# Local attention with score tiles of two PSUM banks, and one POOL add for the rotation

## The chip, the cores and the metric

The kernel runs on one core of a Trainium2 chip. The time of a run is the device time of that core in microseconds (us), and kernels are compared by the median of several runs. The profile is one more execution of the same program, recorded by the hardware profiler. Its engines are PE (matrix products, with PEld for the weight loads beside it), DVE (vector engine), ACT (scalar engine, functions such as Exp and Ln) and POOL (the second vector engine). Each engine works through its own list of instructions in the order in which they were written, and semaphores make one engine wait for another. PSUM, where PE writes, has eight banks of 512 float32 numbers in each of 128 partitions. SBUF holds everything else.

## The reference

The reference is a network of many different blocks on an input of 16 sequences of 256 tokens with 128 channels, 4096 tokens in all. One block, local attention followed by a gated feed-forward net, occurs twice with the same weights, and each occurrence has two layers (`DEPTH`). So local attention is computed four times. Cut to what matters here:

```python
HEADS, DIM_HEAD, WINDOW, QK_SCALE = 8, 64, 64, 8.0

def _layer(x, wqkv, qs, ksc, wo, ...):
    h = shift_token(x)                 # half of the channels come from the token before
    q, k, v = split(h @ wqkv)          # 8 heads of 64 each
    q = l2norm(q) * qs                 # q / clip(norm(q), 1e-12)
    k = l2norm(k) * ksc
    q, k = rotary_xpos(q, k)           # q*cos*scale + rotate_half(q)*sin*scale, k with 1/scale
    o = local_attention(q, k, v)
    x = x + o @ wo
    ...                                # shift, layer norm, feed-forward

def rotate_half(x):
    x1, x2 = jnp.split(x, 2, axis=-1)
    return jnp.concatenate([-x2, x1], axis=-1)

def local_attention(q, k, v):          # windows of 64 tokens, each sees itself and the one before
    ...
    sim = jnp.einsum('bhwid,bhwjd->bhwij', bq * QK_SCALE, bk)
    sim = jnp.where((i < j) | (i > j + WINDOW) | (j == -1), -max, sim)
    return jnp.einsum('bhwij,bhwjd->bhwid', softmax(sim), bv)
```

## The kernel before

The program runs its blocks one after the other. A local layer is `local_attend` (line 3358) followed by `local_ffn`. I number the four calls of `local_attend` layers 1 to 4 in order of time.

**Tiles and slots.** The 4096 tokens are cut into 32 *tiles* of 128 tokens (`NTILE`), so two tiles make one sequence. The work on a tile makes q, k and v ready. The attention itself goes by *slots*, also 32: slot m is sequence m // 2 with four of the eight heads. Eight chunks of 512 tokens (`NCH`) carry the residual, the norm and the output.

**What is done for a tile n.**
- `project`: PE multiplies the tile with the q and the k weights into two `w` banks of PSUM. ACT squares both banks into `sq` (`sq<-ps`). DVE multiplies each bank with the cosine and the sine table (`t<-ps,tab`, four instructions), into `t1` and `t2`. The tables already hold the signs and the scales.
- `rotate`: DVE sums the squares over each head into `ss`, 16 numbers a token (`ss<-sq`), and raises them to at least 1e-24, which is a maximum with a constant tile `least` (`ss<-ss,least`, called the *floor* below). POOL adds `t2` to `t1` with the halves of each head exchanged, in two instructions, one for each half (`t<-t,t`, lines 3408 and 3409).
- `unit`: ACT takes Ln and then Exp of `ss` in place (`ss<-ss`), which gives one over the norm. POOL multiplies `t1` with it (`t<-t,ss`).
- `turn`: PE transposes `t1` into `w` banks (line 508), ACT copies them into `qkt`, and PE makes v in another `w` bank, which ACT copies to SBUF (`v<-ps`).

**What is done for a slot m.**
- `score`: four banks from the group `s`. PE puts the mask into the last two by a product with the identity (line 504), and eight products (line 3447) fill all four. The first two banks hold the scores against the first key tile, 384 numbers each, the other two those against the second, 256 each. DVE takes the minimum of the first two with the mask `see` into `pt` (line 531, two instructions, 384 wide), and ACT takes the exponentials of the other two into `pu` (`pu<-ps`, two instructions, 256 wide).
- `first_weights`: ACT takes the exponential of `pt` in place.
- `weigh`: PE multiplies the weights with v into an `o` bank and sums them by a product with ones (line 3485). The sums go to `pd`, the unused half of the last score bank of the slot that comes next (`spare[3]`); the last slot takes banks for itself.
- `inverse` and `divide`: ACT takes Ln and Exp of `pd`, which gives one over the sum (`rd`), and DVE multiplies the `o` bank with it into `ot`.

`out` multiplies `ot` with the output weights and adds it to the residual, once in four slots. `chunk_steps` has the layer norm of the next part and the token shift of chunks not yet needed (`shift`, three POOL instructions).

**The order.** It is written out by hand. One loop runs m from -9 to 37, and each turn of it calls, where the index is in range: `score(m)`, `weigh(m-1)`, `out`, `turn(m+2)`, `first_weights(m)`, `rotate(m+4)`, `inverse(m-1)` and `divide(m-1)`, `unit(m+4)`, `chunk_steps(m)`, `project(m+5)`. So in one turn a tile is projected five turns before, rotated four turns before and turned two turns before the slot of the same number. The turns with m below 0 have no score yet: I call them the *lead-in* of a layer. In it only tiles are prepared. From slot 0 on each turn has a whole slot as well.

**The banks.** `self.share(w=3, s=4, o=1)` divides the eight banks: three for projections, transposes, v and outputs, four for scores, one for the weighted sum. A tile's next use waits for the instructions that read or wrote it last. `t1` has three buffers, `t2` and `sq` one, `ss` three, `pt`, `pu` and `rd` two.

The helper names in the profile: `tt` is line 531 (DVE), `gt` line 534 (POOL), `act` line 528, `mm` line 504, `tr` line 508. A line there says how an engine was called, not who called it; so the groups are told apart by their tiles.

Of the kernel before, what the change touches and what calls it, by code (L numbers as in the profile page):

```python
# [11 lines left out]
F32, BF16, I32 = mybir.dt.float32, mybir.dt.bfloat16, mybir.dt.int32  # L12
SP = mybir.EngineType.SP
AF = mybir.ActivationFunctionType
ALU = mybir.AluOpType
AX = mybir.AxisListType

P = 128
B, T, C = 16, 256, 128
# [3 lines left out]
NTILE = NT // P  # L23
# [468 lines left out]
class Net:  # L492
# [16 lines left out]

    def bank(self, tag="ps"):  # L510
        return self.psum.tile([P, 512], F32, tag=tag, name="ps", bufs=self.banks[tag])

    @contextmanager
    def share(self, **banks):
# [1135 lines left out]
class Fast(Net):  # L1650
# [1707 lines left out]
    def local_attend(self, w, z, hs, last):  # L3358
# [6 lines left out]
        with ExitStack() as st:  # L3365
            p = self.stage(st, "l1", 1)
# [15 lines left out]
            made, rot, qkt, val, weights, sums, outs, steps, spare = {}, {}, {}, {}, {}, {}, {}, {}, []  # L3382
# [19 lines left out]
            def rotate(n):  # L3402
                sq, t1, t2 = made.pop(n)
                ss = p.tile([P, 16], F32, tag="ss", name="ss", bufs=3)
                nc.vector.tensor_reduce(ss, sq.rearrange("p i (h d) -> p (i h) d", h=8), AX.X, ALU.add)
                self.tt(ss, ss, least, ALU.max)
                a, b = (t.rearrange("p i h a d -> p (i h) a d") for t in (t1, t2))
                for k in range(2):
                    self.gt(a[:, :, k], a[:, :, k], b[:, :, 1 - k], ALU.add)
                rot[n] = t1, ss  # L3410

            def unit(n):
                t1, ss = rot[n]

                self.act(ss, ss, AF.Ln, scale=2.0**20)
                self.act(ss, ss, AF.Exp, scale=-0.5)
                t3 = t1.rearrange("p i h a d -> p (i h) (a d)")
                self.gt(t3, t3, ss[:, :, None].broadcast_to([P, 16, 64]), ALU.mult)

            def turn(n):  # L3420
                b, t = divmod(n, 2)
                if t == 0:
                    qkt[b] = p.tile([P, 2, 4, T], F32, tag="qkt", name="qkt", bufs=2)
                t1, _ = rot.pop(n)
                for i in range(2):
                    pt = self.bank("w")
                    for g in range(4):
                        self.tr(pt[:, g * P : g * P + P], t1[:, i, 2 * g : 2 * g + 2])
                    self.act(qkt[b][:, i, :, t * P : t * P + P], pt.rearrange("p (g t) -> p g t", g=4), AF.Copy)
                pv = self.bank("w")  # L3430
                self.mm(pv, hs[:, n * P : n * P + P], w["qkv"][:, 1024:])
                val[n] = p.tile([P, 512], F32, tag="v", name="v", bufs=6)
                self.act(val[n], pv, AF.Copy)

            def score(m):


                b, hg = divmod(m, 2)
                qt, kt = qkt[b][:, 0], qkt[b][:, 1]
                ps = [self.bank("s") for _ in range(4)]  # L3440
                for bank in ps[2:]:
                    self.mm(self.bt(bank[:, :T]), identb, self.twice(masked), stop=False)

                def product(a, i, t, out):
                    rows, g = slice(64 * a, 64 * a + 64), 2 * hg + i
                    wide = 192 - 64 * t
                    nc.tensor.matmul(
                        out, kt[rows, g, t * P : t * P + P], qt[rows, g, t * P : t * P + wide],
                        start=(i, t) == (0, 0), stop=i == 1, skip_group_check=t == 0,
                    )  # L3450

                for i, t, bank, at in ((0, 0, 0, 0), (1, 0, 0, 192), (0, 1, 2, 0), (1, 1, 2, P)):
                    for a in range(2):
                        product(a, i, t, ps[bank + a][:, at : at + 192 - 64 * t])
                pt = p.tile([P, 2, 384], F32, tag="pt", name="pt", bufs=2)
                pu = p.tile([P, 4, P], F32, tag="pu", name="pu", bufs=2)
                for a in range(2):
                    self.tt(
                        pt[:, a].rearrange("p (i t) -> p i t", i=2), ps[a][:, :384].rearrange("p (i t) -> p i t", i=2),
                        self.twice(w["see"]), ALU.min,  # L3460
                    )
                for a in range(2):
                    self.act(pu[:, a::2], self.bt(ps[2 + a][:, :T]), AF.Exp)
                weights[m] = pt, pu
                spare[:] = ps

            def first_weights(m):
                pt = weights[m][0]
                flat = pt.rearrange("p a t -> p (a t)")
                self.act(flat, flat, AF.Exp)  # L3470

            def weigh(m):


                b, hg = divmod(m, 2)
                pd, po = spare[3][:, T:] if m < NTILE - 1 else self.bank("s")[:, T:], self.bank("o")
                pt, pu = weights.pop(m)
                for half in (0, 1, -1):
                    for t in range(2):
                        wide = 192 - 64 * t  # L3480
                        for r in range(4):
                            i, a = divmod(r, 2)
                            d = (4 * hg + r) * 64 + 32 * half
                            at = max(half, 0) * T + t * P
                            nc.tensor.matmul(
                                (pd if half < 0 else po)[32 * r : 32 * r + 32, at : at + wide],
                                self.ones64[:, :32] if half < 0 else val[2 * b + t][:, d : d + 32],
                                pu[:, r] if t else pt[:, a, i * wide : i * wide + wide],
                                start=t == 0 and half < 1, stop=t == 1 and half != 0, skip_group_check=True,
                            )  # L3490
                sums[m] = pd, po

            def inverse(m):
                pd, po = sums[m]
                rd = p.tile([P, T], F32, tag="rd", name="rd", bufs=2)
                self.act(rd, pd, AF.Ln)
                self.act(rd, rd, AF.Exp, scale=-1.0)
                sums[m] = po, rd

            def divide(m):  # L3500
                b, hg = divmod(m, 2)
                if m % 4 == 0:
                    outs[b // 2] = p.tile([P, 4, CH], F32, tag="ot", name="ot", bufs=1)
                po, rd = sums.pop(m)
                at = b % 2 * T
                self.tt(
                    outs[b // 2][:, 2 * hg : 2 * hg + 2, at : at + T], po.rearrange("p (g t) -> p g t", g=2),
                    self.twice(rd), ALU.mult,
                )

            def out(c):
                pz = self.bank("w")
                ot = outs.pop(c)
                for g in range(4):
                    self.mm(pz, w["wo"][:, g * C : g * C + C], ot[:, g], start=g == 0, stop=g == 3)
                zs = z[:, self.chunk(c)]
                self.tt(zs, zs, pz, ALU.add)

            def within(n, many):
                return 0 <= n < many  # L3520
# [18 lines left out]
                            steps[1] = self.norm_of_half(p, "w", w, hs[:, self.chunk(c)])  # L3539
                        steps[1][i]()  # L3540

            with self.share(w=3, s=4, o=1), self.tc.manual_schedule():
                self.logs()
                for m in range(-9, NTILE + 6):
                    if within(m, NTILE):
                        score(m)
                    if within(m - 1, NTILE):
                        weigh(m - 1)
                    c, rest = divmod(m - 5, 4)
                    if rest == 0 and 0 <= c < NCH:  # L3550
                        out(c)
                    if within(m + 2, NTILE):
                        turn(m + 2)
                    if within(m, NTILE):
                        first_weights(m)
                    if within(m + 4, NTILE):
                        rotate(m + 4)
                    if within(m - 1, NTILE):
                        inverse(m - 1)
                        divide(m - 1)  # L3560
                    if within(m + 4, NTILE):
                        unit(m + 4)
                    chunk_steps(m)
                    if within(m + 5, NTILE):
                        project(m + 5)
# [278 lines left out]
```

## Time and profile before

| | |
|---|---|
| median of 4 runs | 4235.99 us (4234.45 to 4236.53) |
| profiled execution | 4233.97 us, span 4232.2 us from its first to its last instruction |
| mean granted clock of PE over the span | 0.951 |
| busy over the whole span | PE 91%, PEld 52%, DVE 60%, ACT 55%, POOL 44% |

The four layers of local attention lie at these places. A window of slots runs from the score of slot 2 to the end of the last score, slot 31; a lead-in window from DVE's first products of the layer to the score of slot 1.

| layer | lead-in, us | PE busy there | POOL busy there | slots 2 to 31, us | PE busy there |
|---|---|---|---|---|---|
| 1 | 116.50 to 142.25 | 17.88 of 25.75 | 22.51 | 149.13 to 394.70 | 238.91 of 245.57 |
| 2 | 470.50 to 496.30 | 18.55 of 25.80 | 21.27 | 503.15 to 737.50 | 231.49 of 234.35 |
| 3 | 1108.80 to 1134.50 | 18.55 of 25.70 | 21.43 | 1141.30 to 1386.90 | 238.94 of 245.60 |
| 4 | 1462.70 to 1488.30 | 19.28 of 25.60 | 21.20 | 1495.20 to 1729.50 | 231.44 of 234.30 |

Layers 1 and 3 take 11 us longer for their slots than 2 and 4, because their `chunk_steps` carry the first norm of the next layer too.

How the profile is read: a group of instructions is one line, engine and operation, written `out<-in` by the program's tile names, with partitions x elements. In a timeline each row has the start in us, the length, the engine and line, the operation; "x2" is a run of two equal instructions whose lengths are given together, and a bracket at the end is the idle time ahead of it and what ended it. In a list of waits a row gives the idle time, the number of waits and the longest, after the instruction that waited and the one that released it. Windows give the busy time of each engine in a stretch, the number of instructions in brackets, the granted clock (1.00 is full speed) and the share of time in which DMA engines worked.

### The profile page before, as it was taken

How to read it: one execution, taken by the hardware profiler on the slowest of the kernel's cores; microseconds unless marked ns; L12 is line 12 of the kernel's file. 1: busy time of each engine (PE TensorE's matmuls, PEld its weight loads, DVE VectorE, ACT ScalarE, POOL GpSimd, SP SyncE). 2: the span in 40 equal slices, each digit the busy share in tenths (PEclk: the TensorE clock that was granted, in tenths of full speed). 3: DMA queues.
4: the chain of work that ended last, by engine and by line, in shares of the span. 5: the costliest groups of instructions: out<-in, count | busy, mean ns of one | idle time of the engine just before them, and what ended most of it. 6: DMA issues, size and time to landing. Idle time of an engine off the chain costs nothing. (4 is left out here: it accounts for less than half of the span.)

```text
span 4232.2 us, 73089 instructions
## 1 busy us (share of the span) xinstructions
PE 3861.2 (91%) x28742; PEld 2203.3 (52%) x28742; DVE 2557.2 (60%) x4503; ACT 2315.7 (55%) x4485; POOL 1855.0 (44%) x1632
## 2 busy tenths in 40 slices
PE   7999999998899999985989879888999999899978
PEld 3555466464465466454965459543444344455333
DVE  4775676464577477473346633555777677486374
ACT  6666466555766466652456634344555454774532
POOL 4763465232565266225433434454555455321251
PEclk9999999988999999996999979999999999999979
DMA  1800000000000000004920049100000000000000
GB/s 61 344 2 1 11 1 2 20 1 1 20 1 1 3 1 2 1 11 143 318 70 12 16 161 313 42 19 16 1 1 1 3 1 6 10 2 19 6 0 21
DMA packets 78400, 176.38 MB, mean 42 GB/s; under 512 B 12606, under 2 KB 39108, under 8 KB 77920
## 3 DMA queue, kind: packets, MB, share of 16 engines
q1 hardware_dynamic: 65568, 148.40, 10.2%
q0 software_dynamic: 9120, 18.51, 1.2%
q8 instruction: 229, 3.75, 0.4%
q10 hardware_dynamic: 3360, 4.72, 0.3%
q14 instruction: 123, 1.01, 0.1%
HBM read 118.28 MB, written 54.20 MB: 41 GB/s over the span
## 5 line engine op out<-in xcount | busy, mean ns | idle before, releaser
L528 ACT ACTIVATE pt<-ps 128x512 f32<-128x512 f32 x640 | 339.9, 600 | 326.1 <-PE ps L504 324.6
L504 PE MATMUL ps<-hb,w 128*128 128x512 f32 (+1 forms) x960 | 461.3, 614 | 4.0 <-issue 3.3
L504 PE MATMUL ps<-w,hb 128*128 128x512 f32 (+2 forms) x896 | 399.8, 567 | 25.5 <-DVE t L531 19.4
L534 POOL TENSOR_TENSOR t<-t,t 128x512 f32<-128x512 f32 x256 | 319.7, 1270 | 160.2 <-DVE t L531 139.6
L531 DVE TENSOR_TENSOR t<-ps,tab 128x512 f32<-128x512 f32 x512 | 317.6, 681 | 82.5 <-ACT sq L528 79.0
L534 POOL TENSOR_TENSOR t<-t,ss 128x1024 f32<-128x1024 f32 x128 | 243.6, 1903 | 192.4 <-ACT ss L528 191.2
L504 PEld LDWEIGHTS ps<-hb,w 128*128 128x128 f32 (+1 forms) x960 | 179.2, 191 | 260.8 <-issue 223.6
L528 ACT ACTIVATE qkt<-ps 128x512 f32<-128x512 f32 x256 | 140.5, 595 | 290.8 <-PE ps L508 290.8
L531 DVE TENSOR_TENSOR u<-u,ps 128x384 f32<-128x384 f32 (+1 forms) x206 | 121.8, 595 | 277.0 <-PE ps L504 117.4
L531 DVE TENSOR_TENSOR ot<-ps,rd 128x512 f32<-128x512 f32 (+2 forms) x224 | 143.2, 639 | 202.7 <-ACT rd L528 202.7
L534 POOL TENSOR_TENSOR nsq<-ha 128x512 f32<-128x512 f32 x112 | 123.5, 1103 | 317.7 <-ACT ha L528 302.0
L504 PEld LDWEIGHTS ps<-w,hb 128*128 128x128 f32 x896 | 155.3, 192 | 178.4 <-issue 121.6
L534 POOL TENSOR_TENSOR both<-pt 128x1024 f32<-128x1024 f32 x64 | 151.3, 2364 | 199.6 <-DVE pt L531 163.9
L504 PE MATMUL ps<-nsq,ct 128*128 128x512 f32 x368 | 203.0, 634 | 30.2 <-POOL nsq L534 25.7
L504 PE MATMUL ps<-ot,w 128*128 128x512 f32 x448 | 213.6, 611 | 16.8 <-DVE ot L531 9.0
L504 PE MATMUL ps<-xt,w 128*128 128x128 f32 x1704 | 221.1, 280 | 1.6 <-ACT xt L528 1.5
L2199 POOL DMA_INDIRECT back<-y,x x142 | 139.1, 980 | 184.3 <-ACT y L528 61.0
L504 PE MATMUL ps<-u,w 128*128 128x512 f32 (+1 forms) x448 | 215.4, 605 | 3.4 <-POOL u L534 3.4
L504 PEld LDWEIGHTS ps<-xt,w 128*128 128x128 f32 x1704 | 204.9, 194 | 3.2 <-ACT xt L528 2.9
L528 ACT ACTIVATE u<-ps,w 128x512 f32<-128x512 f32 x160 | 107.8, 685 | 177.5 <-PE ps L504 174.9
L3741 POOL DMA_INDIRECT rows<-out,idx x128 | 126.2, 986 | 174.7 <-ACT out L528 125.7
L528 ACT ACTIVATE nrs<-ps,ct 128x512 f32<-128x512 f32 x208 | 139.7, 683 | 99.1 <-PE ps L504 88.7
(362 smaller groups left out, 8903.4 us busy)
## 6 DMA issues: line engine op xcount, KB each, us to landing
w<-in_moe_x SPq DMA_DIRECT2D x142, 533.0 KB
rows<-t SPq DMA_DIRECT2D x64, 520.0 KB
x<-rows SPq DMA_DIRECT2D x142, 65.0 KB
w<-in_local_f SPq DMA_DIRECT2D x8, 659.5 KB
y<-back ACTq DMA_DIRECT2D x16, 256.0 KB
y<-back SPq DMA_DIRECT2D x16, 256.0 KB
w<-in_local_f SPq DMA_DIRECT2D x4, 658.5 KB
back<-y,x POOLq DMA_INDIRECT x142
```

The costliest lines, as they stand in the source:

```text
L504: self.nc.tensor.matmul(out, lhsT, rhs, start=start, stop=stop)
L528: self.nc.scalar.activation(out, in_, func, **kw)
L531: self.nc.vector.tensor_tensor(out, a, b, op)
L534: self.nc.gpsimd.tensor_tensor(out, a, b, op)
L2199: nc.gpsimd.indirect_dma_start(views[i], bass.IndirectOffsetOnAxis(ap=x[:, C : C + 1].bitcast(I32), axis=0), y, None, bounds_check=2 * NT ...
L3741: nc.gpsimd.indirect_dma_start(views[(c * 2 + k) * 4 + t], bass.IndirectOffsetOnAxis(ap=idx[:, k, t : t + 1], axis=0), out[:, k, t], None,)
```

## The change

Four edits, all within the local layers.

- A new helper `banks2` allots a tile of two PSUM banks. `score` takes two of these (`first`, `second`) in place of four single banks, and the share of `s` is two tiles of two banks, in place of four of one. The number of banks is the same.
- The two mask minima become one DVE instruction over 2 x 384 = 768 numbers, which reads both banks of `first`.
- The two exponentials into `pu` become one ACT instruction over 2 x 256 = 512 numbers, which reads both banks of `second`.
- In `rotate`, POOL's two adds of 512 numbers become one of 1024, whose second operand is read with the halves of each head in reverse order.

The order of the calls and the PE instructions stay as they are. The last slot's `weigh` takes the second half of a two-bank tile.

```diff
+    def banks2(self, tag):
+        t = self.psum.tile([P, 2, 512], F32, tag=tag, name="ps", bufs=self.banks[tag])
+        return t
...
                 self.tt(ss, ss, least, ALU.max)
                 a, b = (t.rearrange("p i h a d -> p (i h) a d") for t in (t1, t2))
-                for k in range(2):
-                    self.gt(a[:, :, k], a[:, :, k], b[:, :, 1 - k], ALU.add)
+                self.gt(a, a, b[:, :, ::-1], ALU.add)
                 rot[n] = t1, ss
...
-                ps = [self.bank("s") for _ in range(4)]
+                first, second = self.banks2("s"), self.banks2("s")
+                ps = [first[:, 0], first[:, 1], second[:, 0], second[:, 1]]
...
-                for a in range(2):
-                    self.tt(
-                        pt[:, a].rearrange("p (i t) -> p i t", i=2), ps[a][:, :384].rearrange("p (i t) -> p i t", i=2),
-                        self.twice(w["see"]), ALU.min,
-                    )
-                for a in range(2):
-                    self.act(pu[:, a::2], self.bt(ps[2 + a][:, :T]), AF.Exp)
+                self.tt(
+                    pt.rearrange("p a (i t) -> p a i t", i=2), first[:, :, :384].rearrange("p a (i t) -> p a i t", i=2),
+                    w["see"][:, None, None].broadcast_to([P, 2, 2, 192]), ALU.min,
+                )
+                self.act(pu.rearrange("p (i a) t -> p a i t", a=2), second[:, :, :T].rearrange("p a (i t) -> p a i t", i=2), AF.Exp)
...
-                pd, po = spare[3][:, T:] if m < NTILE - 1 else self.bank("s")[:, T:], self.bank("o")
+                pd, po = spare[3][:, T:] if m < NTILE - 1 else self.banks2("s")[:, 1, T:], self.bank("o")
...
-            with self.share(w=3, s=4, o=1), self.tc.manual_schedule():
+            with self.share(w=3, s=2, o=1), self.tc.manual_schedule():
```

## The prediction

> **What bounds the kernel now.** I read the busy time by stage first. Four local-attention stages run (two local blocks of two layers; I call them layers 1 to 4). The rows below give time, then busy time of PE, PEld, DVE, ACT and POOL, granted clock and DMA: slots 2 to 31 of layer 2, then its lead-in, from the first products on DVE to the score of slot 1.
>
> ```profile
> core 0: us, PE busy (x) PEld busy (x) DVE busy (x) ACT busy (x) POOL busy (x), PEclk, DMA share, GB/s
> 503.15:737.50 234.35, 231.49 (x2378) 145.94 (x2377) 168.53 (x256) 153.69 (x361) 138.69 (x124) 1.00 0.01 2
> ...
> 470.50:496.30 25.80, 18.55 (x70) 8.69 (x69) 21.37 (x32) 12.60 (x29) 21.27 (x17) 0.93 0.12 43
> ```
>
> In the slots PE is busy 231.49 of 234.35 us; DVE, ACT and POOL are at 59 to 72%. The same stretch of all four layers leaves PE idle 19.0 us of 959.8 (6.7, 2.9, 6.7 and 2.9). Instructions saved on the other three engines can win no more than that there. In the lead-in PE has holes and DVE and POOL are busy over 80%: a chain across engines sets the time. Next, what ends PE's stops in the slots of layer 1 (total, times, longest):
>
> ```profile
> PE ps L3447 <- ACT rd L528: 1.9, 2, 1.0
> ...
> PE ps L3485 <- ACT pu L528: 0.8, 5, 0.2
> ```
>
> Third, the timeline of layer 2's lead-in (start, length, engine, line):
>
> ```profile
> 478.08 2.48 POOL L534 TENSOR_TENSOR t<-t,t 128x512 f32<-128x512 f32 x2 [0.54 <-DVE t L531]
> ...
> 479.09 0.28 DVE L531 TENSOR_TENSOR ss<-ss,least 128x16 f32<-128x16 f32 x1
> 479.41 0.46 ACT L528 ACTIVATE ss<-ss 128x16 f32<-128x16 f32 x2 [3.50 <-DVE ss L531]
> 479.77 1.07 ACT L528 ACTIVATE sq<-ps 128x512 f32<-128x512 f32 x2
> 480.39 2.48 DVE L531 TENSOR_TENSOR t<-ps,tab 128x512 f32<-128x512 f32 x4 [1.02 <-ACT sq L528]
> ...
> 488.84 2.49 POOL L534 TENSOR_TENSOR t<-t,t 128x512 f32<-128x512 f32 x2
> 488.91 1.23 DVE L531 TENSOR_TENSOR ss<-ss,least 128x16 f32<-128x16 f32 x1
> ...
> 493.58 2.84 PE L504 MATMUL ps<-w,hb 128*128 128x512 f32 x6 [0.25 <-ACT qkt L528]
> ```
>
> This is a loop per tile: DVE's four products, its reduce, its floor `ss<-ss,least`, ACT's Ln and Exp of ss, ACT's square for the next tile, DVE's next products. The floor is the delicate link. It reads two SBUF tiles, and its length says how it fares beside POOL:
>
> ```profile
> L531 DVE TENSOR_TENSOR ss<-ss,least x128: 174/585/1228, 120.2 to 1706.8; 128x16 f32<-128x16 f32 x128
> ...
> L528 ACT ACTIVATE pu<-ps x256: 365/386/402, 138.3 to 1731.5; 128x256 f32<-128x256 f32 x128
> ```
>
> Alone it takes 0.174 us. At 488.91 it began 0.07 after one of POOL's two adds (2.49 us the pair, so about 1.25 each) and ended at 490.14, when that add was over: blocked for the whole instruction. At 479.09 it came near the end of the first add and slipped through the seam before the second. A longer POOL instruction blocks for its whole length as well (layer 1, steady state): the three-operand instruction below takes 0.74 at 381.35, with no POOL work beside it, and 2.30 behind POOL's 1.90 product.
>
> ```profile
> 275.82 1.90 POOL L534 TENSOR_TENSOR t<-t,ss 128x1024 f32<-128x1024 f32 x1 [2.04 <-ACT ss L528]
> ...
> 275.97 2.30 DVE L543 SCALAR_TENSOR_TENSOR hb<-hb,w,nrs 128x512 f32<-128x512 f32 x1
> ```
>
> **The change, part by part.** *POOL's add.* Two adds become one of 1024 elements. Prices, from the groups of POOL (mean ns after the busy time):
>
> ```profile
> L534 POOL TENSOR_TENSOR t<-t,t 128x512 f32<-128x512 f32 x256 | 319.7, 1270 | 160.2 <-DVE t L531 139.6 <-PE ps L504 10.6 <-PE ps L508 9.1
> L534 POOL TENSOR_TENSOR t<-t,ss 128x1024 f32<-128x1024 f32 x128 | 243.6, 1903 | 192.4 <-ACT ss L528 191.2
> L534 POOL TENSOR_TENSOR both<-pt 128x1024 f32<-128x1024 f32 x64 | 151.3, 2364 | 199.6 <-DVE pt L531 163.9 <-ACT pt L528 35.7
> ...
> L534 POOL TENSOR_TENSOR vs<-vs,sg 128x512 f32<-128x512 f32 x16 | 25.2, 1575 | 32.4 <-ACT sg L528 32.4
> ```
>
> No row has an operand read with its halves swapped. I take 2.36 us from `both<-pt`: two full tensors, as here. Low end 1.90 (the second operand of `t<-t,ss` is one value repeated); high end 2 x 1.575 - 0.22 = 2.93, the slowest 512-element add twice, less about 0.11 of fixed cost each way. POOL saves 2.48 - 2.36 = 0.12 us a tile, 15 us in 128 tiles, worth nothing in the slots, where POOL is at 59%. But the seam is gone. In tile 1 of layer 2 the floor ended at 479.09 + 0.28 = 479.37; now it ends 0.03 after the add (as 488.84 + 1.27 against 490.14 shows), at 478.08 + 2.36 + 0.03 = 480.47: 1.10 late. The floor of tile 3 was blocked by the first add alone; it is 1.09 late too. Late next: ACT's Ln and Exp, and in ACT's order behind them the squares, then DVE's products, which free the w banks that PE waits for.
>
> *What reaches PE.* In layer 2, tiles 0, 1 and 2 make tile 3's products 3 x 1.09 = 3.3 late. Tile 3's add then waits for POOL, which finishes tile 2's product and the shift 2.66 late, so tile 3's floor ends 2.66 + 1.09 = 3.75 late, and tile 4's products (491.21 to 493.69) as well. The matmul of v at 493.58 needs the bank that they free: PE stands there now (0.25 idle) and will stand 3.75 longer. Layer 3 shows the same rows. In layers 1 and 4 ACT already waits 0.3 and 0.5 in the third tile, which absorbs part; done the same way I get 3.65. Sum: 3.75 + 3.75 + 3.65 + 3.65 = **+14.8 us**. From slot 1 on PE is the limit and nothing gives it back. No more is added in the slots: there the floor's new end lies at least 0.2 us ahead of ACT's turn for ss in every slot (tightest in slot 0 of each layer: 493.84 + 2.39 = 496.23 against 496.46). That is the cover; an add over 2.6 us would use it up.
>
> [...]
>
> *The second tile's exponential.* Two of 256 elements take 0.66 together (269.62), one of 512 about 0.60 (the lone `v<-ps` copies). PE's 20 stops on `pu` (5 a layer, 0.17 each) shrink by 0.06: **-1.2** (from 0 to -3.4, all of them).
>
> *The waits on the score banks.* Pairs of banks are now released together. Before, the first score product waited for DVE's minimum and the second for ACT's Ln of `rd`; now the first waits for Ln. Where PE stops there for 0.95 (twice a layer), one more product is queued behind it: eight take 1.37, so 0.17 each, 8 stops: **+1.4** (0 to +2.8). The wait for the minimum moves to the first mask matmul; the minimum ended over 4 us earlier, so nothing.
>
> *The mask minimum.* Two take 1.01 us; one of 768 elements, extrapolated from 546 ns at 384 and 680 at 512 (1.05 ns an element), about 0.9. DVE's 0.1 a slot lies under PE's matmuls; uncovered it would be 13 us. The stops that name DVE come after a DVE instruction blocked by POOL. Zero (0 to -1.2).
>
> Sum: 14.8 - 1.2 + 1.4 = +15.0. The profiled execution took 4233.97 (span 4232.2 and 1.8 around it), so 4249.0; the runs' median lies 2.0 above it: **4251.0**. With the ends: floors 0.64 to 1.67 late against 1.09 make 8.7 to 22.7 of the 14.8; with the small terms +4.1 to +25.5, that is 4240 to 4261.
>
> **Rivals.** (a) *The floor gets through before the long add ends.* Then the lead-ins cost 0 and the small terms leave +0.2: 4236, not slower. For: no row shows this add. Against: the 2.30 row. It decides if the floor's median in the lead-ins stays near 0.2 us. 0.14. (b) *The saved ACT and DVE time opens PE's stops.* Half of the 19.0 would be -9.5: 4226.5. Against: ACT's chain ahead of Ln in those stops (qkt copies, v, exp of pt) holds none of the merged instructions. 0.04. (c) *Part of the delay is absorbed*, because lead-ins run at a granted clock of 0.87 to 0.93, and PE, half-clocked, is itself late: 2 us a layer less, +7: 4243. 0.08. (d) *The swapped operand costs more than any row*, say 3.1 us an add: 1.84 x 14.8/1.09 = +25: 4261. 0.05.
>
> **The numbers.** Forecast 0.69. What counts as no change is within 0.2%, 8.5 us. Slower takes the forecast but its lowest end (0.67), (d) and a little of (c): 0.74. Same takes (a), most of (c) and that end: 0.21. Faster: 0.05. The range 4240 to 4261 holds the forecast, (c) and (d) and leaves out (a) and (b), 0.18.
>
> **What would show it.** One POOL `t<-t,t` of 1024 elements near 2.36; in the lead-ins floors of about 1.3 us in place of 0.2; products of one tile to the next 6.0 apart, not 4.9; the mask matmul of slot 1 some 3.7 later after the lead-in's start; the slots' length unchanged within 0.5 us a layer. It is wrong if floors in the lead-in stay at 0.2, or if the lead-ins grow and the slots shrink by as much.

## The result and the profile after

| | before | changed |
|---|---|---|
| median, first comparison | 4235.73 us (54 runs) | 4240.08 us (33 runs) |
| ratio, 95% interval | | 1.0014 (1.0008 to 1.0019) |
| profiled execution | 4233.97, span 4232.2 | 4239.18, span 4237.4 |
| four local layers in the profile, first DVE products to the score of slot 31 | 1090.26 | 1101.33 |
| lead-ins among them, to the score of slot 2 | 130.52 | 143.05 |
| slots 2 to 31 among them | 959.75 | 958.28 |

By the ratio the changed kernel is slower by 5.9 us (3.4 to 8.0); the medians lie 4.35 apart. That is less than the 8.5 us taken as no change, and the median of 4240.08 is at the low edge of the range. Inside the local layers the cost is 11.1 us: 12.5 lost in the lead-ins, 1.5 won in the slots. About half of the 11 doesn't show in the whole time.

Here and below "the score" of a slot stands for the start of its first mask product. The windows of slots ahead of the prediction end there too, at the start of slot 31's score and not at its end, which comes 1.7 us later. Lead-ins are measured here to the score of slot 2, one slot further than there. In three of the experiments below one run stood far above the rest (6155 to 14991 us); it counts in none of the ratios.

First the page's head, and the group of POOL's add and the floor among the instructions on `ss` (min/median/max in ns). A changed line has moved down by 4 in the changed kernel (531 is 535, 534 is 538).

```profile
span 4237.4 us, 72705 instructions
...
L538 POOL TENSOR_TENSOR t<-t,t 128x1024 f32<-128x1024 f32 x128 | 302.3, 2362 | 166.6 <-DVE t L535 145.8
```

```profile
L535 DVE TENSOR_TENSOR ss<-ss,least x128: 174/541/1684, 122.0 to 1710.6; 128x16 f32<-128x16 f32 x128
```

The add takes 2.362 us, the value taken from `both<-pt` (2.364); here reading an operand with its halves swapped costs nothing more. Next the timeline of layer 2's lead-in:

```profile
477.71 2.34 POOL L538 TENSOR_TENSOR t<-t,t 128x1024 f32<-128x1024 f32 x1 [6.02 <-PE ps L504]
478.79 1.29 DVE L535 TENSOR_TENSOR ss<-ss,least 128x16 f32<-128x16 f32 x1
480.18 0.46 ACT L532 ACTIVATE ss<-ss 128x16 f32<-128x16 f32 x2 [4.33 <-DVE ss L535]
480.54 1.06 ACT L532 ACTIVATE sq<-ps 128x512 f32<-128x512 f32 x2
...
481.15 2.48 DVE L535 TENSOR_TENSOR t<-ps,tab 128x512 f32<-128x512 f32 x4 [1.07 <-ACT sq L532]
...
483.78 2.34 POOL L538 TENSOR_TENSOR t<-t,t 128x1024 f32<-128x1024 f32 x1 [1.10 <-DVE t L535]
...
484.80 1.36 DVE L535 TENSOR_TENSOR ss<-ss,least 128x16 f32<-128x16 f32 x1
...
487.17 2.48 DVE L535 TENSOR_TENSOR t<-ps,tab 128x512 f32<-128x512 f32 x4 [1.01 <-ACT sq L532]
```

The floor starts 1.08 us after the add's start, while the add runs, and ends at 480.08, 0.03 after the add. ACT's Ln follows 0.10 later, then the squares, then DVE's next products. From products to products it is 487.17 - 481.15 = 6.02, where before it was 4.94. The windows of layer 2 (time, then busy time of PE, PEld, DVE, ACT, POOL, granted clock, DMA), lead-in and slots:

```profile
475.08:510.89 35.81, 27.04 (x149) 14.27 (x148) 30.04 (x38) 17.07 (x38) 24.89 (x14) 0.86 0.09 31
510.89:744.86 233.97, 229.89 (x2378) 145.33 (x2376) 171.38 (x227) 151.78 (x332) 135.17 (x98) 1.00 0.01 2
```

To the score of slot 2 the lead-in takes 35.81 us against 32.69, the slots 233.97 against 234.33.

### The profile page after: what moved, and what is told of

Its sections match the earlier page's. It is cut to its first block, busy times and chain, and to the rows that moved or that the text cites. A ratio compares the mean times of both kernels' runs of the same rounds, so it can differ in the third digit from the quotient of the medians.

```text
span 4237.4 us, 72705 instructions
## 1 busy us (share of the span) xinstructions
PE 3848.9 (91%) x28742; PEld 2196.7 (52%) x28742; DVE 2579.7 (61%) x4375; ACT 2305.6 (54%) x4357; POOL 1836.0 (43%) x1504
## 3 DMA queue, kind: packets, MB, share of 16 engines
q8 instruction: 229, 3.75, 0.4%
q10 hardware_dynamic: 3360, 4.72, 0.3%
## 5 line engine op out<-in xcount | busy, mean ns | idle before, releaser
L538 POOL TENSOR_TENSOR t<-t,t 128x1024 f32<-128x1024 f32 x128 | 302.3, 2362 | 166.6 <-DVE t L535 145.8
L538 POOL TENSOR_TENSOR nsq<-ha 128x512 f32<-128x512 f32 x112 | 123.3, 1101 | 319.4 <-ACT ha L532 303.5
```

The source lines that it names most:

```text
L538: self.nc.gpsimd.tensor_tensor(out, a, b, op)
```

## The experiments

Twelve kernels ran, in three groups: the first four of the table, the next four and the last four. Each is compared with the kernel before on the same chip in the same group; the chip of the first and third group runs both some 24 us faster behind the local layers, so whole times are compared inside a group only. "Local" is the sum of the four layers in the profile, "lead-ins" and "slots" its two parts as in the table above.

| kernel | local | lead-ins | slots | median, before | ratio (95%) |
|---|---|---|---|---|---|
| add_split | 1088.95 | 130.59 | 958.35 | 4211.65, 4214.04 | 0.9998 (0.9989 to 1.0007) |
| add_only | 1102.40 | 142.86 | 959.54 | 4223.12, 4214.04 | 1.0023 (1.0013 to 1.0032) |
| floor_scalar | 1101.23 | 142.87 | 958.36 | 4217.50, 4214.04 | 1.0010 (1.0000 to 1.0019) |
| no_floor | 1090.42 | 127.33 | 963.10 | 4212.38, 4214.04 | 0.9997 (0.9988 to 1.0006) |
| no_floor_leadin | 1086.24 | 127.73 | 958.51 | 4235.82, 4239.65 | 0.9993 (0.9984 to 1.0002) |
| banks_only | 1090.92 | 131.32 | 959.60 | one run, 4240.45 | |
| after_again | 1101.28 | 142.90 | 958.38 | 4238.00, 4239.65 | 1.0003 (0.9994 to 1.0013) |
| before_again | 1091.87 | 132.06 | 959.81 | 4239.09, 4239.65 | 1.0001 (0.9991 to 1.0011) |
| after_third | 1101.51 | 143.15 | 958.36 | 4216.21, 4214.35 | 1.0005 (0.9996 to 1.0013) |
| after_fourth | 1101.40 | 143.04 | 958.36 | 4223.91, 4214.35 | 1.0021 (1.0012 to 1.0030) |
| before_third | 1090.81 | 131.25 | 959.56 | 4214.38, 4214.35 | 0.9996 (0.9987 to 1.0005) |
| before_fourth | 1090.84 | 131.29 | 959.54 | 4215.13, 4214.35 | 1.0002 (0.9993 to 1.0011) |

### Which part of the change costs

add_split undoes POOL's merge alone:

```diff
-                self.gt(a, a, b[:, :, ::-1], ALU.add)
+                for k in range(2):
+                    self.gt(a[:, :, k], a[:, :, k], b[:, :, 1 - k], ALU.add)
```

> The changed kernel with POOL's add in two instructions again; the two-bank tiles stay. Yardstick: the four local layers, each from its first DVE products to the score of its last slot, took 1090.3 us together before and 1101.3 after the change. Theory (the long add blocks the floor in the lead-ins): lead-in floors back at 0.2 to 0.3 us in tiles 0 to 2 of a layer, products of one tile to the next 4.9 us apart again, the four layers about 1088.8 (1090.3 less the 1.45 that the slots gained after the change). Rival (the two-bank tiles and their shared release cost the time): no change against the changed kernel, 1101. Whole time: theory 11 to 13 us below the changed kernel, if the clock grants the same elsewhere.

add_only makes the opposite edit, in the kernel before:

```diff
-                for k in range(2):
-                    self.gt(a[:, :, k], a[:, :, k], b[:, :, 1 - k], ALU.add)
+                self.gt(a, a, b[:, :, ::-1], ALU.add)
```

> The kernel before with POOL's merged add alone; single banks, two minima and two exponentials as before. Theory (the long add alone costs): lead-in floors of 1.2 to 1.7 us, products 6.0 us apart, the four local layers about 1090.3 + 12.5 = 1102.8 us. Rival (the two-bank tiles cost): 1090.

The local times are 1088.95 and 1102.40, within 0.4 us of what the theory gave; the rival gave 1101 and 1090. So the merged add costs 12.3 to 12.5 us, all of it in the lead-ins, and the rest of the change (two-bank tiles, merged minimum, merged exponential) gains 1.4, all of it in the slots. Executions of the unedited kernel before differ in their lead-ins, 130.52 to 132.06 in four profiles against 142.90 to 143.15, so the cost is 11.8 by the means. The changed kernel itself didn't run in this group; the 11 to 13 us forecast for the whole time of add_split stay open. The timeline of add_split shows the seam at work again:

```profile
477.56 2.48 POOL L538 TENSOR_TENSOR t<-t,t 128x512 f32<-128x512 f32 x2 [0.55 <-DVE t L535]
...
478.57 0.29 DVE L535 TENSOR_TENSOR ss<-ss,least 128x16 f32<-128x16 f32 x1
478.89 0.46 ACT L532 ACTIVATE ss<-ss 128x16 f32<-128x16 f32 x2 [3.51 <-DVE ss L535]
```

The floor ends at 478.86, 1.18 us before POOL's pair of adds does.

### What the floor needs to get past POOL

floor_scalar gives the floor one SBUF input and a constant:

```diff
-                self.tt(ss, ss, least, ALU.max)
+                self.ts(ss, ss, 1e-24, ALU.max)
```

> The changed kernel with the floor as an instruction of one SBUF input and a constant (maximum of ss with 1e-24) in place of two SBUF inputs. If only instructions with two SBUF inputs are blocked by a running POOL instruction: floors of about 0.17 us everywhere, also beside the merged add, and the four local layers at 1088.8 us or a little less. If any DVE instruction from SBUF to SBUF is blocked: floors of 1.2 to 1.7 us in the lead-ins and 1101.

The second case came true: the lead-ins stay at 142.87. The timeline of floor_scalar:

```profile
480.99 1.21 DVE L3407 TENSOR_REDUCE ss<-sq 128x16 f32<-128x1024 f32 x1
...
481.22 2.35 POOL L538 TENSOR_TENSOR t<-t,t 128x1024 f32<-128x1024 f32 x1 [6.07 <-PE ps L504]
482.23 1.36 DVE L542 TENSOR_SCALAR ss<-ss 128x16 f32<-128x16 f32 x1
```

With one SBUF input the floor is blocked to the add's end as well (482.23 + 1.36 = 483.59, the add's end 483.57). The reduce, which starts before the add and overlaps it, keeps its 1.21 us (1.20 to 1.21 in all 128 of this run), and the add beside it its 2.35. What makes the floor wait is not shown.

no_floor takes the floor off DVE. Ln gets 1e-24 (times its scale) as a bias, so the computation adds 1e-24 where the kernel took a maximum:

```diff
-            least = one([P, 16], "least")
-            nc.gpsimd.memset(least, 1e-24)
+            least = one([P, 1], "least")
+            nc.gpsimd.memset(least, 1e-24 * 2.0**20)
...
-                self.tt(ss, ss, least, ALU.max)
...
-                self.act(ss, ss, AF.Ln, scale=2.0**20)
+                self.act(ss, ss, AF.Ln, bias=least, scale=2.0**20)
```

> The changed kernel without the floor: ACT's Ln takes ss with 1e-24 added (as its bias) in place of the maximum with 1e-24. Theory (the floor is the link through which the add delays the lead-in): the merged add is harmless, the loop of a tile loses the floor too, products 4.9 less about 0.3 us apart, the four local layers at about 1088.8 - 4 = 1085 us, and the whole time 5 us below the kernel before. Rival (POOL's longer add delays the chain by itself, or the two-bank tiles do): 1098 to 1101.

Half of it came true. With the merged add in place the lead-ins fall to 127.33, 15.7 below the changed kernel and 3.2 below the kernel before; products are 4.72 to 4.80 apart in the first two tiles. So the add harms the lead-in through the floor; a kernel with two adds and no floor, which would show whether anything is left beside that, did not run. But the slots grew from 958.3 to 963.1, which no theory had. The instructions on `ss` in no_floor:

```profile
L532 ACT ACTIVATE ss<-ss,least x128: 291/292/309, 120.0 to 1709.5; 128x16 f32<-128x16 f32 x128
L532 ACT ACTIVATE ss<-ss x128: 215/215/218, 120.3 to 1709.8; 128x16 f32<-128x16 f32 x128
```

With a bias Ln takes 0.292 us in place of 0.215, and ACT reaches the squares about 0.1 later. In some slots `pu` comes as much later and PE waits for it (slots of 7.00 us became 7.10, of 8.09 became 8.18; those of 10.53 and 7.74 stayed). no_floor_leadin therefore drops the floor in tiles 0 to 3 alone:

```diff
-                self.tt(ss, ss, least, ALU.max)
+                if n >= 4:
+                    self.tt(ss, ss, least, ALU.max)
...
+                if n < 4:
+                    self.act(ss, ss, AF.Ln, bias=small, scale=2.0**20)
+                else:
+                    self.act(ss, ss, AF.Ln, scale=2.0**20)
```

> The changed kernel, without the floor in the lead-in alone: tiles 0 to 3 of a layer add 1e-24 as the bias of ACT's Ln, tiles 4 to 31 keep the maximum on DVE. no_floor gained 15.7 us in the lead-ins over the changed kernel (127.3 against 143.05) and lost 4.8 in the slots (963.1 against 958.3), where each Ln with a bias took 0.29 us and not 0.215 and what stands behind it on ACT came 0.1 later. Theory (those are two separate effects): lead-ins 127.3, slots 958.3, the four layers 1085.7, that is 4.6 below the kernel before and 15.6 below the changed one. Rival (the slots are longer because tiles came out of the lead-in earlier, or for want of the floor): slots stay at 963.

Lead-ins 127.73 and slots 958.51: two separate effects. That the slots of no_floor grew by the bias, and not because no floor stands there, is read from its timeline; no run separates the two. In the profile this version's local layers are 4.0 us below the kernel before, and its median is the lower one by 3.8 us, but the ratio 0.9993 (0.9984 to 1.0002) doesn't exclude 1. No version was shown to beat both kernels.

### The small terms in the slots

banks_only has the two-bank tiles and their shared release, with two minima, two exponentials and two adds. Against the kernel before, without the helper and the last slot's `weigh`, which are as in the change:

```diff
-                ps = [self.bank("s") for _ in range(4)]
+                first, second = self.banks2("s"), self.banks2("s")
+                ps = [first[:, 0], first[:, 1], second[:, 0], second[:, 1]]
...
-            with self.share(w=3, s=4, o=1), self.tc.manual_schedule():
+            with self.share(w=3, s=2, o=1), self.tc.manual_schedule():
```

> The kernel before with two-bank score tiles alone: two minima, two exponentials and two adds as before, but a pair of banks is released together. My prediction had +1.4 us for that wait, 8 stops with one more product behind it, and -1.2 for the exponential. add_split measured -1.4 in the slots for the whole. If the wait costs nothing and the exponential gains 1.4: slots 959.8 us (960.0 at most) as before. If the wait costs 1.4 and the exponential gains 2.8: 961.2.

The waits of PE in the slots of layer 1 (total, times, longest), first of banks_only, then of the changed kernel, whose list has no row for `pu`:

```profile
PE ps L3452 <- ACT rd L532: 3.6, 3, 1.5
...
PE ps L3490 <- ACT pu L532: 0.8, 5, 0.2
```

```profile
PE ps L3451 <- ACT rd L532: 3.6, 3, 1.5
```

The stops at the score products grew from 1.9 to 3.6 us in all and from two to three, as in the changed kernel, and yet the slots take 959.60, as before. A stop begins earlier because the first product waits now, but it ends when Ln ends, as it did, and the products that had run before the stop cost nothing behind it: in slots 29 and 30 of layer 2 the products go on 1.85 us after the slot's first mask product and end at 3.21 in the kernel before, at 1.85 and 3.22 in banks_only. The wait is worth 0 in the slots. The 1.4 us that they gain come from the merged exponential and minimum together; no run has one without the other. The missing row for `pu` points to the exponential. The lead-ins of banks_only are 0.1 to 0.25 longer in each layer than in the first profile of the kernel before, which add_split doesn't show; that is open.

### Where half of the cost goes

after_again and before_again are the two kernels unedited, to learn whether the missing 5 us are chance.

> The changed kernel once more, unedited, for its time outside the local layers. Inside, the change adds 11.1 us; the first comparison of the whole time gave only 5.9 (ratio 1.0014, interval 1.0008 to 1.0019). Theory A (the rest differs by the clock granted from execution to execution, not by the change): the ratio nears 1.0026, and the 371 us between layers 2 and 3 are as often long as short in kernels with the merged add and in those without. Theory B (some 5 us are given back later in every execution): the ratio stays at 1.0014, and that stretch is shorter than before each time (362, not 371).

> The kernel before once more, unedited, as the control for after_again: ratio 1 within 0.0015; local layers 1090.3 us. Theory A: the stretch between layers 2 and 3 takes anything from 362 to 373 us, with the time lost to a lowered clock in it. Theory B: 371 again.

Neither theory fits as it stood: the ratio fell to 1.0003, yet the stretch between layers 2 and 3 took 373.1 us this time. That stretch, the same instructions in both kernels, holds the difference. Windows of 55 us at the same place in it, 90 us after the end of layer 2, first in the kernel before, then in the changed kernel, then in after_again:

```profile
827.47:882.47 55.00, 53.49 (x426) 39.97 (x419) 37.51 (x77) 24.65 (x37) 18.52 (x21) 0.72 0.03 12
```

```profile
834.86:889.86 55.00, 49.61 (x502) 37.50 (x494) 44.51 (x90) 30.24 (x47) 21.39 (x24) 0.94 0.03 13
```

```profile
836.44:891.44 55.00, 53.84 (x433) 40.71 (x434) 38.91 (x78) 24.82 (x38) 19.48 (x22) 0.72 0.03 12
```

The granted clock is 0.94 in one profile of the changed kernel and 0.72 in the other; with it PE gets through 502 instructions in the same 55 us in place of 433. In the clock's records the granted share is either 1 or 0.5, and every stretch at 0.5 begins on a grid of 3.4133 us, which goes on through the whole execution: the 45 to 55 such stretches of each profile (53 in each of the first two) lie within 0.001 us of it. I took from each profile the place of the end of layer 2 on that grid, and the clock lost (time by 1 less the granted share) up to layer 3. The last four kernels, both again unedited, tested the rule drawn from the first ten profiles. Three kernels spend 1.05 us more in the unedited feed-forward part behind a layer, so 1.05 is added to their places.

> The changed kernel, unedited, for one more profile and more times. In ten profiles so far the clock's lowered stretches begin on a grid of 3.4133 us, and the clock lost between layers 2 and 3 went with where the end of layer 2 (the score of its last slot) lay on that grid: 20 to 27 us lost at 0.24, 0.28 and 0.48 us past a grid line, 32 to 36 at 0.14, 0.54, 1.0 and later (three kernels whose feed-forward part ran 1.05 us longer are counted at their end plus 1.05). Theory C (place on the grid decides): the same rule in this profile. Theory C2 (besides, the long lead-ins tie the end of layer 2 to the grid): its place lies within 0.5 of a grid line, as in the four profiles with the merged add (0.24, 0.48, 3.06, 3.20), so that the cheap places come more often than the 1 in 7 of chance. Rival (chance alone): anywhere.

> As after_third: theory C, 20 to 27 us lost at a place from 0.2 to 0.5, else 32 to 36; theory C2, a place within 0.5 of a grid line; chance, anywhere. Ratio of the times of both together: 1.0026 if nothing is given back, near 1.001 if about half is, as in the two comparisons so far (1.0014 and 1.0003).

> The kernel before, unedited, as the control. Theory C: 20 to 27 us of clock lost between layers 2 and 3 only at a place from 0.2 to 0.5 past a grid line, else 32 to 36. Theory C2: its place is anywhere (1.62 and 2.74 so far). Ratio 1 within 0.0012.

> The kernel before once more, as before_third: 20 to 27 us of clock lost between layers 2 and 3 only at a place from 0.2 to 0.5 past a grid line (theory C), its place anywhere (theory C2), ratio 1 within 0.0012.

In the list of the expectation, 0.54 is no_floor_leadin's place before its 1.05 is added, by mistake; it should read 1.59. All fourteen:

| profile | place, us | clock lost | stretch, us |
|---|---|---|---|
| changed | 0.48 | 20.5 | 362.2 |
| after_third | 0.47 | 20.5 | 362.2 |
| after_fourth | 0.55 | 20.5 | 362.1 |
| add_only | 0.24 | 23.9 | 365.8 |
| floor_scalar | 3.06 | 35.8 | 373.3 |
| after_again | 3.20 | 35.8 | 373.1 |
| before | 1.62 | 32.4 | 371.3 |
| before_third | 1.70 | 32.4 | 371.2 |
| before_fourth | 1.67 | 35.8 | 374.6 |
| before_again | 2.74 | 32.4 | 373.6 |
| add_split | 1.04 | 32.4 | 371.9 |
| banks_only (with 1.05) | 0.19 | 32.4 | 373.8 |
| no_floor (with 1.05) | 0.33 | 27.3 | 370.2 |
| no_floor_leadin (with 1.05) | 1.59 | 35.8 | 375.8 |

Theory C as it was stated (20 to 27 us lost at 0.2 to 0.5, else 32 to 36) held in three of the four new profiles; after_fourth, at 0.55, lost 20.5. With the bound moved to 0.6 afterwards all fourteen profiles fit, but these bounds are drawn from the same profiles, and no run moves the place alone: the table shows that place and lost clock go together, not that the one causes the other. C2 missed by as little: all six profiles with the merged add and the floor behind it lie within 0.55 of a grid line (0.5 was said), and of the eight others two do, both only by the 1.05.

The traces show where the places come from. Layer 1 begins 1.2 to 2.0 us past a grid line in all fourteen profiles, though the executions themselves begin at 0.2 to 3.2. From there to the end of layer 2 the changed kernel takes 626.5 to 626.7 us in its four profiles, the kernel before 621.0 to 622.6. So the places are not drawn evenly from 3.41 us, and six of six near a line is no evidence of a tie by itself: the changed kernel's three cheap profiles began layer 1 at 1.8 to 2.0, its dear one at 1.4. And layer 3 begins 0.83 to 0.89 past a line in all fourteen, so that the stretch makes up for the place at its start and differs beyond that by whole periods. What brings the kernel back onto the grid is not shown.

The means of the stretch are 366.5 us over those six profiles (362 to 373) and 372.5 over the five others with the same feed-forward time (371 to 375). So about 6 of the 10.4 us that the local layers cost (means of the four profiles of each kernel, 1101.4 and 1090.95) come back there, roughly, from so few profiles.

The whole times show it too. The runs of after_fourth fall into two groups, 4211.4 and 4216.0, and nine from 4222.6 to 4227.9; after_third has eight from 4206.5 to 4217.4 and three from 4223.3 to 4225.2. In after_again three of eleven lie above 4246, the profiled one with its long stretch among them, and in the first comparison seven of 33 above 4249; the three profiles with the short stretch are all of the lower group. The same program on the same chip thus gave medians of 4216.2 and 4223.9 against 4214.35, by which group came more often. The four comparisons of the changed kernel, weighted by the inverse square of their intervals' widths, give 1.0012 (1.0008 to 1.0015), that is 5.0 us; but the four differ by more than their intervals allow, so this interval is too narrow.

What the place does to the clock was not tested and stays open. So does how often the cheap place comes: 44 of the changed kernel's 66 runs lie in the lower group, but from 2 of 11 to 26 of 33 by comparison.

## Why the prediction was right, and where it was off

**The mechanism was right, and most of its numbers.** The add at 2.36 us (2.362), the floor blocked to its end (1.22 to 1.36 us in tiles 0 to 2, where 1.3 was said), products 6.0 apart (5.95 to 6.19), a loop 1.09 later each tile: in layer 2 the floors of tiles 0, 1, 2 and 3 end 1.07, 2.15, 3.24 and 3.69 us later after the lead-in's start, against 1.09, 2.18, 3.3 and 3.75. The fifth tile's products are 3.69 late. The undoing and the lone edit (add_split, add_only) show that nothing else in the change costs.

**The step from tile 4's products to PE was mis-sized.** It had the matmul of v wait for the bank that the products free, so that slot 1 comes 3.75 late, 14.8 us in all. Slot 1 came 3.12 late in layer 2, and the lead-ins lost 12.5. The timeline there:

```profile
499.47 0.66 PE L508 MATMUL ps<-ct,t 128*128 128x128 f32 x4
499.53 2.48 DVE L535 TENSOR_TENSOR t<-ps,tab 128x512 f32<-128x512 f32 x4 [1.07 <-ACT sq L532]
...
500.97 0.63 PE L508 MATMUL ps<-ct,t 128*128 128x128 f32 x4 [0.84 <-ACT qkt L532]
...
501.43 2.74 PE L504 MATMUL ps<-w,hb 128*128 128x512 f32 x6
...
504.01 0.38 PE L504 MATMUL ps<-masked,identb 128*128 128x256 bf16 x2
```

v starts at 501.43 without a wait, 0.58 before the fourth product ends at 502.01. What stops PE is the second group of transposes at 500.97. Two things end just ahead of that: the first copy into `qkt` at 500.96 (500.35 + 0.61 in the same timeline), which the profile names, and the second of the four products at 500.82. Either way the fourth product is not it. The prediction's own row shows as much: there v starts at 493.58, released by `qkt`, 0.11 before the products' end at 493.69. The 0.6 us a layer are 2.3 of the 3.9 us by which the sum of 15.0 was too high.

**The wait on the score banks, +1.4, was 0**, as banks_only shows: a longer stop that ends at the same time is no loss. **The exponential, -1.2, was -1.4** with whatever the mask minimum did, which the prediction put at nothing and no run separated. For that minimum the prediction's 1.05 ns an element gives 0.95 us at 768 elements, not 0.9; it took 0.95. The high end of the add's price takes off 0.22 of fixed cost, about the length of two of POOL's memsets of `least` (16 numbers, 0.113 us each in the kernel before); two adds against one give 2 x 1.270 - 2.364 = 0.18 by the mean rows. With these, 12.5 + 0 - 1.4 = 11.1 us.

**What lies outside the stage was taken to stay.** The sum was set on one execution's 4233.97, and the only place for the clock was rival (c), inside the lead-ins. There it absorbed little: the lead-ins lost 3.1 to 3.2 us a layer. But the unedited stretch behind layer 2 gave back about 6 of the 10.4 us, in step with where the change had moved the end of layer 2 on the clock's grid. That step wasn't in the prediction at all, and it turns 4247 into about 4241. The median of 4240.08 is in the range by 0.08 us, which is luck, and by the bound of 8.5 us it counts as no change, which had 0.21 against 0.74 for slower.

**Of the rivals**, (a) falls with the floors of 1.3 us, (b) with the slots' 1.4 us, and (d) with the add's 2.362 us.

## What to carry to other kernels

Two short instructions on one engine can be worth more than one long one, where another engine's small instruction gets through the seam between them (here DVE's floor took 0.29 us beside two POOL adds, 1.29 beside one); before merging, look for what runs beside the merged one and is blocked for its whole length, and ask which loop that sits in. A longer wait in the list of waits is a loss only if its end moved (here 3.6 us of stops in place of 1.9 cost nothing). And a few us lost in an early stage can come back in part in a later one whose granted clock varies (here 0.94 and 0.72 over the same 55 us): read the edited stage by itself, and repeat the unedited kernel before believing a whole time.

## What the runs showed of the hardware

- A maximum of 16 elements from SBUF with a constant is blocked by a POOL add just as one with two SBUF inputs is: 1.30 to 1.37 against 1.22 to 1.36 us in tiles 0 to 2, where an unblocked floor takes 0.174.
- An Ln of 16 elements takes 0.292 us with a bias from SBUF and 0.215 without; where every Ln had one, 120 slots took 4.8 us more.
- In all fourteen profiles half-clocked stretches begin on a grid of 3.4133 us, and profiles whose unedited stretch began 0.47 to 0.55 us past a grid line lost 12 to 15 us less clock in it than those at 1.0 to 3.2.
- In banks_only, no_floor and no_floor_leadin the unedited feed-forward part behind a layer took 76.8 us in place of 75.8, behind layers 1 and 3, and 1.05 us more behind layer 2. Why is open.
